# Layer 1 of a gated cross-attention stack: the last key tile joins the row sums on VectorE in about half of the groups

## The chip, the cores and the metric

The kernel runs on one core of one Trainium2 chip. The metric is the device time of one execution in microseconds (us); given is the median of several runs. Beside it there is one profiled execution, whose rows of instructions are used for all reasoning about single steps. In the profile PE is TensorE's matmuls, PEld its weight loads, DVE VectorE, ACT ScalarE, POOL GpSimd and SP the engine that issues most DMAs.

## The reference, cut to what matters

Two layers process 8 sequences of 512 tokens with 256 channels. Each layer is an attention part, gated with tanh(g) and added to x, and then a quantized feed-forward part. The change lies in the attention of layer 1, which has 16 heads of width 32 and two blocks for each sequence: a1 (self attention, with the mask applied after the softmax) and a2 (cross attention on the context, no mask):

```python
a = jax.nn.softmax(jnp.einsum('bhsd,bhtd->bhst', q, k) * D ** (-0.5), axis=-1)
if causal:
    mask = (jnp.arange(t)[None, :] > jnp.arange(s)[:, None]).astype(a.dtype)
    a = a * mask
o = jnp.einsum('bhst,bhtd->bhsd', a, v)
```

The softmax is normalized over all 512 keys, also in the masked block. So for each query and head the kernel needs the sum of 512 exponentials, and separately the product of the exponentials, masked or not, with v. Behind each block follow a product with li1, a layer norm, and an MLP of width 1024 (li2, GELU, li3).

## The kernel before, in words

**Groups.** Four heads make a group, so each of the 16 blocks (8 sequences times a1 and a2) has four groups, 64 in all. Scores are computed transposed: keys on the partitions, queries along the row. A group runs over four tiles of 128 keys (n = 0 to 3; last to first in a1). Each tile has two steps in `steps1` (line 2532):

- `front` (line 2547): four score products on PE, one per head, into two double banks of PSUM (line 2555); two exponentials of 128 x 1024 on ACT into a tile pt of 128 x 4 x 512 (line 2558). In a1, POOL also makes dg, a masked copy of the diagonal 128 columns (line 2562), and only the unmasked columns left of it and dg are multiplied with v.
- `back` (line 2570): the products of v with the parts, four heads side by side on the array (line 2579), into the bank ov. Beside them DVE gathers the row sums: at n = 1 it adds the tiles of n = 0 and 1 into acc (line 2587), at n = 2 it adds the third (line 2589). At n = 3 the sum over the partitions is made on PE: a product of acc with a matrix of ones, and a second of the last pt with ones, into one bank sm (lines 2593 to 2596). DVE turns sm, takes the reciprocal, spreads it and scales ov into oT (lines 2602 to 2607).

The ring of pt has three tiles (`PTS`), acc has one. Three PSUM banks (pool m1a, line 2100) serve all other products of layer 1, the bank sm among them; they come free when ACT or DVE has read them.

**The order.** PE, ACT, DVE, POOL and SP each run one fixed order, made when the program is built. `weave_all` (line 2152) keeps the attention steps and a number of streams: `first` and `last` (feed-forward parts of layers 0 and 1), `pair1` (queries and keys of a group), `pre1` (norms and values), `mlp1`, `keys2_rest` (keys and values of the context) and some small ones. Each has a due place counted in blocks: a base, plus a share of its work done. `Pace` (line 812) models when each engine is free and each tile done. Of the candidates that could start now, or within `soon`, the one with the smallest due place is issued next; if there is none, the one that can start first. Fronts are at most two ahead of backs. `back_at` (line 2611) says when a back may start; for n = 3 it is when pt, v and acc are done and a bank is free. All bases and shares stand in `SET`, `FIRST_AT` and `LAST_AT` (lines 29 to 74); `weave_timed` (line 1229) does the same for layer 0. Where PE would stand idle for long, `warm` (line 1282) puts in products that nobody reads.

**The keys of the context.** `keys2` (line 2025) makes keys and values of the first `KEYS_FIRST` sequences (five) during the feed-forward part of layer 0, and `keys2_rest` (line 2036) the others in layer 1, in tiles of the pt ring. Each takes eight products, eight evacuations, two stores to DRAM on SP's queue (lines 2068 and 2076) and a load from POOL's queue (lines 2022 and 2049). `mlp1` and the loads of the values wait until all are made.

Of the kernel before, what the change touches and what calls it, by code (L numbers as in the profile page):

```python
# [11 lines left out]
ALU = mybir.AluOpType  # L12
# [6 lines left out]
NT = T // P  # L19
# [6 lines left out]
MAGIC = 12582912.0  # L26
NEG = -1.0e30
ROWS = ((0, 1), (2, 3, 4), (5, 6, 7))
FIRST_AT = (-2.25, -0.57, 3.08, 3.44, 3.8, 6.44, 6.45, 6.2)
LAST_AT = (4.16, 6.04, 7.56, 7.63, 10.89, 12.49, 15.6)  # L30
PTS = 3
SET = dict(
    pairs0=2.7,
    post0=0.793,
    values0=0.0,
    few0=0.334,
    load1=1.367,
    norm0=0.547,
    ctx0=1.479,
    next0=1.066,  # L40
    gains_at=0.873,
    ready_at=-0.998,
    keys0=8.15,
    ease=1.612,
    zact=1.28,
    hold=0.158,
    keys0_at=-0.077,
    range_total=8.18,
    range_share=0.949,
    warm=0.888,  # L50
    conv_at=-1.687,
    soon=0.467,
    change0=0,
    change1=0,
    first=1.293,
    first_lag=4.549,
    last=0.367,
    last_total=7.836,
    last_lag=0.711,
    mlp0=0.488,  # L60
    mlp1=0.767,
    mlp0_at=1.131,
    mlp1_at=1.351,
    pre=1.286,
    pre_at=-1.524,
    pre_lag=0.783,
    pair=0.189,
    pair_at=-0.254,
    keys=0.466,
    keys_at=-0.443,  # L70
    back=1.031,
    tail_at=15.68,
    half_at=0.13,
)
KEYS_FIRST = 5


_COLS = [
# [995 lines left out]
class Fast(General):  # L1074
# [789 lines left out]
    def layer0_ffn(self):  # L1864
# [5 lines left out]
        with (  # L1870
# [18 lines left out]
            for b in range(B):  # L1889
                streams.append(Stream(self.ready0(b), 1.0, 0.1, b + SET["ready_at"]))  # L1890
                streams.append(Stream(self.range0(b), SET["range_total"], SET["range_share"], b))
            streams.append(Stream(self.chain(*(self.keys2(b) for b in range(KEYS_FIRST))), 64.0, SET["keys0"], SET["keys0_at"]))
            self.weave_timed([], streams)
# [131 lines left out]
    def keys2(self, b):  # L2025

        work, w = self.work, self.w1s[1]
        cT = self.cTs.pop(0)
        if b + 3 < KEYS_FIRST:
            self.load_cT(b + 3)  # L2030
# [5 lines left out]
    def keys2_rest(self):  # L2036
# [9 lines left out]
        def load(b):  # L2046
            if b < B:
                cTs[b] = self.early.tile([P, 1, T], F32, tag=f"x3T{b % 2}", name="cT")
                nc.gpsimd.dma_start(cTs[b][:, 0, :], self.cd[b])

        load(KEYS_FIRST)
        load(KEYS_FIRST + 1)
        yield WAIT
        for b in range(KEYS_FIRST, B):
            k = work.tile([P, 4, T], F32, tag="pt", name="k2", bufs=PTS)
# [34 lines left out]
    def layer1_xattn(self):  # L2090
        nc, tc = self.nc, self.tc
        with (
# [24 lines left out]

            for k, b in zip(FIRST_AT, range(B)):
                few.append(Stream(self.first(b), 3.8, SET["first"], k, SET["first_lag"]))
                if b == 1:  # L2120
                    few.append(Stream(self.load_mlp(), 1.0, 1.0, k))
            for k, b in zip(LAST_AT, range(B - 1)):
                few.append(Stream(self.last(b), SET["last_total"], SET["last"], k, SET["last_lag"]))
# [18 lines left out]
            self.keys_done, self.x0_read = False, 0  # L2142
            keys = [Stream(rest, 8.0 * (B - KEYS_FIRST), SET["keys"], SET["keys_at"])]
            self.weave_all(
# [387 lines left out]
    def steps1(self, b, blk):  # L2532

        nc, work, q, pace = self.nc, self.work, self.seqs[b], self.pace
        strict = blk == 0
        order = list(reversed(range(NT))) if strict else list(range(NT))
        slot = self.slot_of(b, blk)
        st = {}  # L2540

        def front_at(g):
            if ("QK", blk, g) not in q or slot and ("vt", blk) not in q:
                return 1e9
            return max(pace.when([Pace.name(t) for t in q["QK", blk, g]]), pace.place("st", 2))

        def front(g, n):
            kt = order[n]
            self.fronts += 1
            QT, KT = q["QK", blk, g]  # L2550
            diag = slice(kt * P, (kt + 1) * P)
            pss = [self.st.tile([P, 2, T], F32, tag="st", name="ps_s") for _ in range(2)][::-1]
            for j in (2, 3, 0, 1):
                r = slice(32 * j, 32 * j + 32)
                self.mm(pss[j // 2][:, j % 2, :], KT[r, diag], QT[r, :])
            pt = work.tile([P, 4, T], F32, tag="pt", name="pt", bufs=PTS)
            for jp in (1, 0):
                nc.scalar.activation(pt[:, 2 * jp : 2 * jp + 2, :], pss[jp], AF.Exp)  # L2558
            parts = [(pt, slice(0, T))]
            if strict:  # L2560
                dg = work.tile([P, 4, P], F32, tag="dg", name="dg", bufs=2)
                nc.gpsimd.affine_select(  # L2562
                    out=dg, in_=pt[:, :, diag], compare_op=ALU.is_gt, fill=0.0,
                    base=0, pattern=[[0, 4], [-1, P]], channel_multiplier=1,
                )
                parts = [(pt, slice(0, kt * P))] if kt else []
                parts.append((dg, diag))
            st[g, n] = (kt, pt, parts)

        def back(g, n):  # L2570
            self.backs += 1
            kt, pt, parts = st.pop((g, n))
            if n == 0:
                st["ov"] = self.ovp.tile([P, T], F32, tag="ov1", name="ov")
            ov = st["ov"]
            for i, (p, cols) in enumerate(parts):
                for j in (2, 3, 0, 1):
                    h = 4 * g + j
                    self.mm(
                        ov[32 * j : 32 * j + 32, cols], q["vt", blk][:, kt, 32 * h : 32 * h + 32],  # L2580
                        p[:, j, : cols.stop - cols.start],
                        n == 0 and i == 0, n == NT - 1 and i == len(parts) - 1,
                    )

            if n == 1:
                st["acc"] = work.tile([P, 4, T], F32, tag="acc", name="acc")
                nc.vector.tensor_tensor(st["acc"], st["pt"], pt, ALU.add)  # L2587
            elif n == 2:
                nc.vector.tensor_tensor(st["acc"], st["acc"], pt, ALU.add)  # L2589
            st["pt"] = pt  # L2590
            if n < NT - 1:
                return
            sm = self.bank()
            for k, t in enumerate((st["acc"], pt)):
                for j in (2, 3, 0, 1):
                    self.mm(sm[32 * j : 32 * j + 32, :], self.ones, t[:, j, :], k == 0, k == 1)

            if g == 0:
                st["recs"] = work.tile([P, 4, 16], F32, tag="recs", name="recs", bufs=2)
            rec = st["recs"][:, g, :]  # L2600
            rt = work.tile([P, 16, 32], F32, tag="rt", name="rt", bufs=1)
            nc.vector.transpose(rt.rearrange("p b d -> p (b d)"), sm)
            nc.vector.reciprocal(rec, rt[:, :, 0])
            rb = work.tile([P, T], F32, tag="rt", name="rb", bufs=1)
            nc.vector.transpose(rb, rec.unsqueeze(2).to_broadcast([P, 16, 32]))
            oT = q["oT", blk, g] = work.tile([P, T], F32, tag="oT", name="oT", bufs=5)
            nc.vector.tensor_tensor(oT, ov, rb, ALU.mult)  # L2607
            if g == 3:
                self.seen(st["recs"])

        def back_at(g, n):

            if n == NT - 1 and min(self.li1s) < (4 * slot + g - 1) // 4 or ("vt", blk) not in q:
                return 1e9
            _, pt, parts = st[g, n]
            t = pace.when([Pace.name(pt), Pace.name(q["vt", blk])] + [Pace.name(p) for p, _ in parts])
            if n == 0:
                return max(t, pace.place("ov1"))
            return max(t, pace.when([Pace.name(st["acc"])]), pace.place("m1")) if n == NT - 1 else t

        return [
            (lambda g=g: front_at(g), lambda g=g, n=n: back_at(g, n),
             lambda g=g, n=n: front(g, n), lambda g=g, n=n: back(g, n))
            for g in range(4) for n in range(NT)
        ]
# [337 lines left out]
```

## Time and profile before

| what | before |
|---|---|
| median of the runs | 2548.03 us (2546.71 to 2550.03, 3 runs) |
| profiled execution, its own time | 2552.98 us |
| its span, first to last instruction | 2551.2 us |
| mean granted TensorE clock | 0.98 of full speed |
| records of matmuls of pt with ones | 512, mean 606 ns |
| records of matmuls of acc with ones | 512, mean 607 ns |
| adds into acc on DVE | 64 of 2356 ns and 64 of 2419 ns in the mean |
| masked copies dg on POOL | 128, mean 1003 ns |

One product of four heads leaves eight matmul records, so 512 records are 64 groups. A row names the source line, the engine, the operation, "out<-in" by the program's names, the shapes and the count. A helper's line stands for all its callers: matmuls carry the lines of `mm` (1211 and 1215). In a row, "busy, mean" are the summed time and the mean of one; "<-" names what ended the idle time before it. Rows of the timeline begin with the start and the length in us.

### The profile page before, as it was taken

What the parts mean: (1) busy time and instruction counts of PE and PEld (TensorE: products, weight loads), DVE (VectorE), ACT (ScalarE), POOL (GpSimd) and SP (SyncE); (2) the same over time, 40 slices, a digit from 0 to 9 for tenths busy, and PEclk for the clock granted to TensorE, in tenths of its full rate; (3) what the DMA queues carried; (4) which work ended last, traced back from release to release, by engine and by line L of the source; (5) the groups of instructions that cost most, each with busy time, mean ns of one, the idle gap of its engine ahead of it and who ended that gap; (6) DMA issues with size and microseconds to landing.
All of it is one profiled execution on the core that took longest, in us unless ns stands there. A gap on an engine that the chain in (4) does not pass through costs nothing.

```text
span 2551.2 us, 68484 instructions
## 1 busy us (share of the span) xinstructions
PE 2401.7 (94%) x30510; PEld 1018.0 (40%) x30510; DVE 1718.6 (67%) x3118; ACT 1457.3 (57%) x1744; POOL 645.8 (25%) x684
## 2 busy tenths in 40 slices
PE   9999999999979998999999999999999989999975
PEld 3333333333423343334444434444444444344543
DVE  5544555444685656574877786778877877777867
ACT  5666776666685555555555555565555554565421
POOL 1211121111432444231423332222323441111100
PEclk9999999999999999999999999999999999999988
DMA  3101120000284302301201012331020102201000
GB/s 123 39 18 55 55 80 26 19 29 18 105 366 162 125 10 92 113 31 48 83 31 51 10 58 84 133 109 34 31 83 16 35 18 72 80 27 50 27 27 19
DMA packets 70640, 165.36 MB, mean 65 GB/s; under 512 B 5952, under 2 KB 32960, under 8 KB 63296
## 3 DMA queue, kind: packets, MB, share of 16 engines
q1 hardware_dynamic: 68960, 157.18, 17.7%
q8 instruction: 241, 3.95, 0.6%
q0 software_dynamic: 1088, 3.67, 0.5%
q14 instruction: 63, 0.52, 0.1%
q10 hardware_dynamic: 288, 0.05, 0.0%
HBM read 100.06 MB, written 60.82 MB: 63 GB/s over the span
## 4 chain that ended last, share of the span: by engine, by line


## 5 line engine op out<-in xcount | busy, mean ns | idle before, releaser
L2558 ACT ACTIVATE pt<-ps_s 128x1024 f32<-128x1024 f32 x512 | 496.2, 1021 | 342.5 <-PE ps_s L1215 257.4
L1215 PE MATMUL ps_s<-QT,KT 32*128 32x512 f32 (+3 forms) x4096 | 590.0, 598 | 22.6 <-ACT pt L2558 11.7
L1675 ACT ACTIVATE pt<-ps_s 128x1024 f32<-128x1024 f32 (+1 forms) x448 | 406.1, 961 | 198.7 <-PE ps_s L1215 191.9
L1215 PEld LDWEIGHTS ps_s<-QT,KT 32*128 32x128 f32 x4096 | 195.5, 183 | 352.0 <-issue 194.9
L1211 PE MATMUL ps<-x3T,li 128*32 128x256 f32 x4096 | 244.6, 384 | 5.4 <-DVE x3T L2483 4.2
L1211 PE MATMUL ps<-li,hD 128*32 128x256 f32 x4096 | 234.8, 382 | 2.0 <-ACT hD L2505 2.0
L1215 PE MATMUL ov<-pt,v 128*32 128x512 f32 (+3 forms) x2048 | 225.5, 522 | 5.6 <-POOL pt L1678 5.6
L2562 POOL TENSOR_SCALAR_AFFINE_SELECT dg<-pt 128x512 f32<-128x512 f32 x128 | 128.3, 1003 | 393.9 <-ACT pt L2558 392.1
L2315 POOL TENSOR_SCALAR mv<-mv 128x2 f32<-128x2 f32 (+1 forms) x104 | 67.0, 644 | 624.2 <-DVE mv L2310 620.2
L1215 PE MATMUL ov<-pt,vt 128*32 128x512 f32 (+3 forms) x1792 | 195.5, 508 | 13.1 <-DVE oT L2607 12.3
L1678 POOL TENSOR_SCALAR_AFFINE_SELECT pt<-pt 128x512 f32<-128x512 f32 (+1 forms) x96 | 83.1, 869 | 389.4 <-ACT pt L1675 389.4
L1211 PEld LDWEIGHTS ps<-li,hD 128*32 128x32 f32 x4096 | 130.5, 110 | 108.1 <-issue 14.8
L1211 PEld LDWEIGHTS ps<-x3T,li 128*32 128x32 f32 x4096 | 128.7, 111 | 110.5 <-issue 22.9
L2589 DVE TENSOR_TENSOR acc<-acc,pt 128x2048 f32<-128x2048 f32 x64 | 154.8, 2419 | 2.1 <-ACT pt L2558 1.5
L2587 DVE TENSOR_TENSOR acc<-pt 128x2048 f32<-128x2048 f32 x64 | 150.8, 2356 | 1.2 <-ACT pt L2558 1.2
L2082 ACT ACTIVATE hD<-ps,cols 128x256 f32<-128x256 f32 x131 | 57.6, 471 | 132.3 <-PE ps L1211 115.6
L1211 PE MATMUL ps<-zT,a_wq 128*32 128x512 f32 x1024 | 123.7, 602 | 2.4 <-DVE zT L2399 1.7
L1211 PE MATMUL ps<-li,oT 128*32 128x256 f32 x2048 | 123.0, 380 | 2.0 <-DVE oT L2607 1.3
L1701 DVE STREAM_TRANSPOSE ot<-ov 128x512 f32<-128x512 f32 x64 | 45.7, 714 | 109.3 <-PE ov L1215 109.3
L2681 DVE SCALAR_TENSOR_TENSOR hF<-hp,cols,hF 128x256 f32<-128x256 f32 x176 | 90.7, 515 | 27.8 <-ACT hF L2672 22.8
L1215 PEld LDWEIGHTS ov<-pt,v 128*32 128x32 f32 x2048 | 49.2, 108 | 148.0 <-issue 91.8
L2316 POOL TENSOR_TENSOR mv<-mv,mhalf 128x2 f32<-128x2 f32 (+1 forms) x120 | 99.6, 830 | 10.0
(350 smaller groups left out, 3562.6 us busy)
## 6 DMA issues: line engine op xcount, KB each, us to landing
hd<-h SPq DMA_DIRECT2D x14, 1024.0 KB, 6.7
hF<-hd SPq DMA_DIRECT2D x14, 1024.0 KB, 6.6
li<-in_w_a_dram SPq DMA_DIRECT2D x12, 1024.0 KB, 5.0
xF<-xd SPq DMA_DIRECT2D x21, 512.0 KB, 3.6
kd<-k SPq DMA_DIRECT2D x8, 1024.0 KB, 5.3
vd<-v SPq DMA_DIRECT2D x8, 1024.0 KB, 6.1
res<-rd SPq DMA_DIRECT2D x32, 256.0 KB, 2.8
vt<-vd SPq DMA_DIRECT2D x8, 1024.0 KB, 5.5
```

Source lines behind the costliest of these rows:

```text
L1211: self.nc.tensor.matmul(out[j : j + 32], lhsT[:, j : j + 32], rhs, start=start, stop=stop, skip_group_check=True)
L1215: self.nc.tensor.matmul(out, lhsT, rhs, start=start, stop=stop, skip_group_check=True)
L1675: nc.scalar.activation(pt[:, 2 * jp : 2 * jp + 2, :at], pss[jp][:, :, :at], AF.Exp)
L1678: nc.gpsimd.affine_select(out=diag, in_=diag, compare_op=ALU.is_ge, fill=0.0, base=0, pattern=[[0, 4], [0, len(kts)], [1, P]], channel_mul ...
L2082: self.nc.scalar.activation(out, ps, AF.Identity, bias=bias)
L2315: nc.gpsimd.tensor_scalar(rstd, mv[:, :, 1], EPS, None, ALU.add)
L2316: nc.gpsimd.tensor_tensor(rstd, rstd, self.mhalf[:, :nt], ALU.pow)
L2558: nc.scalar.activation(pt[:, 2 * jp : 2 * jp + 2, :], pss[jp], AF.Exp)
L2562: nc.gpsimd.affine_select(out=dg, in_=pt[:, :, diag], compare_op=ALU.is_gt, fill=0.0, base=0, pattern=[[0, 4], [-1, P]], channel_multiplier=1,
L2587: nc.vector.tensor_tensor(st["acc"], st["pt"], pt, ALU.add)
L2589: nc.vector.tensor_tensor(st["acc"], st["acc"], pt, ALU.add)
L2681: nc.vector.scalar_tensor_tensor(a, hp[:, half + k : half + k + n], self.col("conv_w", 3 * f + k), a, ALU.mult, ALU.add)
```

## The change

A new step `fold` adds the last pt into acc on DVE. It is tried twice: when the front of n = 3 has been issued, and after the add of n = 2. It needs both to have been issued, and it is done only if, by the plan's model, the add could start less than 3.5 us after the time at which PE becomes free. Where it was done, only acc is multiplied with ones; otherwise the two products remain. Which groups are folded is so decided when the program is built. The back of n = 3 may be issued 0.951 us before acc is done by the model. Nearly all numbers of the order are new, and `KEYS_FIRST` is 4, so one sequence's keys move to `keys2_rest`.

```diff
-FIRST_AT = (-2.25, -0.57, 3.08, 3.44, 3.8, 6.44, 6.45, 6.2)
-LAST_AT = (4.16, 6.04, 7.56, 7.63, 10.89, 12.49, 15.6)
+FIRST_AT = (-3.49, -0.02, 1.23, 2.56, 3.8, 6.79, 6.79, 6.17)
+LAST_AT = (3.99, 4.61, 6.9, 8.97, 11.78, 11.79, 15.6)
 SET = dict(
-    pairs0=2.7,
+    ones_lead=0.951,
+    ones_at=-3.5,
+    pairs0=3.004,
...
-    range_total=8.18,
-    range_share=0.949,
-    warm=0.888,
+    range_total=10.676,
+    range_share=1.373,
+    warm=0.656,
...
-    keys=0.466,
-    keys_at=-0.443,
+    keys=0.57,
+    keys_at=0.432,
...
-KEYS_FIRST = 5
+KEYS_FIRST = 4
...
             st[g, n] = (kt, pt, parts)
+            if n == NT - 1:
+                fold(g)
+
+        def fold(g):
+            if (g, NT - 1) not in st or st.get("folded") != (g, False):
+                return
+            pt = st[g, NT - 1][1]
+            at = pace.when([Pace.name(pt), Pace.name(st["acc"])])
+            if max(pace.free["DVE"], at) < pace.free["PE"] - SET["ones_at"]:
+                nc.vector.tensor_tensor(st["acc"], st["acc"], pt, ALU.add)
+                st["folded"] = g, True
...
                 nc.vector.tensor_tensor(st["acc"], st["acc"], pt, ALU.add)
+                st["folded"] = g, False
+                fold(g)
...
-            for k, t in enumerate((st["acc"], pt)):
+            terms = (st["acc"],) if st["folded"][1] else (st["acc"], pt)
+            for k, t in enumerate(terms):
                 for j in (2, 3, 0, 1):
-                    self.mm(sm[32 * j : 32 * j + 32, :], self.ones, t[:, j, :], k == 0, k == 1)
+                    self.mm(
+                        sm[32 * j : 32 * j + 32, :], self.ones, t[:, j, :],
+                        k == 0, k == len(terms) - 1,
+                    )
...
-            return max(t, pace.when([Pace.name(st["acc"])]), pace.place("m1")) if n == NT - 1 else t
+            return max(t, pace.when([Pace.name(st["acc"])]) - SET["ones_lead"], pace.place("m1")) if n == NT - 1 else t
```

More of the change, by code (lines that the diff above doesn't have):

```diff
@@ L28 @@
 ROWS = ((0, 1), (2, 3, 4), (5, 6, 7))
-FIRST_AT = (-2.25, -0.57, 3.08, 3.44, 3.8, 6.44, 6.45, 6.2)
-LAST_AT = (4.16, 6.04, 7.56, 7.63, 10.89, 12.49, 15.6)
+FIRST_AT = (-3.49, -0.02, 1.23, 2.56, 3.8, 6.79, 6.79, 6.17)
+LAST_AT = (3.99, 4.61, 6.9, 8.97, 11.78, 11.79, 15.6)
 PTS = 3
 SET = dict(
-    pairs0=2.7,
-    post0=0.793,
+    ones_lead=0.951,
+    ones_at=-3.5,
+    pairs0=3.004,
+    post0=0.995,
     values0=0.0,
[L36 to L39, printed above, removed]
+    few0=0.314,
+    load1=1.481,
+    norm0=0.045,
+    ctx0=2.216,
     next0=1.066,
[L41 to L47, printed above, removed]
-    range_total=8.18,
-    range_share=0.949,
-    warm=0.888,
-    conv_at=-1.687,
-    soon=0.467,
+    gains_at=0.94,
+    ready_at=-0.991,
+    keys0=8.019,
+    ease=1.509,
+    zact=1.418,
+    hold=0.54,
+    keys0_at=0.086,
+    range_total=10.676,
+    range_share=1.373,
+    warm=0.656,
+    conv_at=-1.489,
+    soon=0.459,
     change0=0,
     change1=0,
-    first=1.293,
-    first_lag=4.549,
-    last=0.367,
+    first=1.28,
+    first_lag=6.683,
+    last=0.301,
     last_total=7.836,
-    last_lag=0.711,
+    last_lag=0.672,
     mlp0=0.488,
@@ L63 @@
     mlp1_at=1.351,
-    pre=1.286,
-    pre_at=-1.524,
+    pre=1.139,
+    pre_at=-1.432,
     pre_lag=0.783,
-    pair=0.189,
+    pair=0.186,
     pair_at=-0.254,
-    keys=0.466,
-    keys_at=-0.443,
-    back=1.031,
-    tail_at=15.68,
+    keys=0.57,
+    keys_at=0.432,
+    back=1.001,
+    tail_at=15.748,
     half_at=0.13,
 )
-KEYS_FIRST = 5
+KEYS_FIRST = 4
 _COLS = [
```

## The prediction

> **What bounds the kernel now.** The page's head and its first two parts come first: which engine is busiest, and in which part of the span.
>
> ```profile
> span 2551.2 us, 68484 instructions
> PE 2401.7 (94%) x30510; PEld 1018.0 (40%) x30510; DVE 1718.6 (67%) x3118; ACT 1457.3 (57%) x1744; POOL 645.8 (25%) x684
> ...
> PE   9999999999979998999999999999999989999975
> DVE  5544555444685656574877786778877877777867
> ```
>
> PE is full nearly everywhere. DVE (VectorE) takes 4 or 5 tenths in layer 0 and 7 or 8 in layer 1. The chain of waits is empty in this profile, so busy times by stage take its place (start:end, length, then busy us per engine, granted clock, DMA):
>
> ```profile
> 0.00:660.00 660.00, 647.30 (x6590) 231.71 (x6594) 330.00 (x737) 440.96 (x499) 119.64 (x150) 1.00 0.14 46
> 660.00:800.00 140.00, 120.54 (x1428) 49.92 (x1424) 109.80 (x143) 99.05 (x156) 53.44 (x69) 0.93 0.66 263
> 800.00:2395.00 1595.00, 1522.43 (x20517) 669.04 (x20517) 1160.23 (x1989) 881.49 (x1023) 461.02 (x447) 0.99 0.18 59
> 2395.00:2551.00 156.00, 111.46 (x1994) 67.37 (x1983) 118.58 (x252) 35.77 (x67) 11.71 (x19) 0.87 0.08 25
> ```
>
> The third row holds all 64 groups of layer 1. PE idles 1595 - 1522.4 = 72.6 us in it (5%), DVE 434.8 us (27%). PE is the bound there, though not alone. The waits of PE in that stage say for whom (us in total, times, longest):
>
> ```profile
> PE ov L1215 <- POOL dg L2562: 15.6, 16, 3.1
> PE ov L1215 <- DVE oT L2607: 12.3, 15, 1.3
> PE ps_s L1215 <- ACT pt L2558: 11.7, 20, 1.8
> ```
>
> All rows on DVE together make about 36 us. No one wait is long: taking PE work away should shorten the span unless new waits fill the hole.
>
> **What is removed.** The end of one group on PE, from the timeline (start, length):
>
> ```profile
> 1656.85 1.03 PE L1215 MATMUL ov<-pt,vt 128*32 128x512 f32 x8
> 1657.70 1.03 PE L1215 MATMUL ps<-acc,ones 128*32 128x512 f32 x8
> 1658.56 1.03 PE L1215 MATMUL ps<-pt,ones 128*32 128x512 f32 x8
> ```
>
> The price is not the 1.03 us of the row, since neighbours overlap, but the distance between starts: 0.86 us. A folded group loses the third row. "About half" I take as 32 of 64: 32 x 0.86 = 27.5 us of PE (28 to 38 groups: 24 to 33). To see whether half is credible I read in the timeline, for each group, the end of its last exponential, the end of its second add, and the start of the product with acc. The second add ends after the exponential in 59 of 64 groups (median 1.8 us), so DVE has just become free. A further add of 2.35 us would end before the present start of the first sum product in 38 groups, and at most 2.05 us after it in the other 26. Half is what fits without delay.
>
> **What is added.** 32 more adds. Their cost is that of the two existing adds (ns, min/median/max):
>
> ```profile
> L2587 DVE TENSOR_TENSOR acc<-pt x64: 2257/2283/3357, 814.2 to 2379.4; 128x2048 f32<-128x2048 f32 x64
> L2589 DVE TENSOR_TENSOR acc<-acc,pt x64: 2257/2281/3365, 816.6 to 2383.5; 128x2048 f32<-128x2048 f32 x64
> ```
>
> The mean of L2589 on the page is 2419 ns, so 32 x 2.42 = 77 us, and DVE goes from 1160 to 1237 us of 1595, 78%. It has the room, and the cover is the PE work woven between exponential and sum (median 5.4 us). What leaks through:
>
> (a) DVE takes its work in order. The new add waits for the second exponential of the last key tile; behind it stand evacuations of the three banks, for which PE waits. Below nothing is possible only through the planner's other choices, which (c) holds. The low end is 0. The high end is a full add per fold, 32 x 2.28 = 73 us. Nearest row: 36 us of PE waits on 1160 us of DVE work, 0.031 us per us; 77 us would give 2.4 us. Waits grow faster than load, so I double it: +5 us.
>
> (b) In the self-attention block (half the groups, so some 16 folds) the mask's copy dg on POOL is released by the same exponential as the new add. An existing collision:
>
> ```profile
> 1999.53 2.28 DVE L2587 TENSOR_TENSOR acc<-pt 128x2048 f32<-128x2048 f32 x1
> 1999.73 2.58 POOL L2562 TENSOR_SCALAR_AFFINE_SELECT dg<-pt 128x512 f32<-128x512 f32 x1 [2.55 <-ACT pt L2558]
> ```
>
> The select's median is 635 ns, here it ends 0.5 us after the add. The Trainium skill (SBUF — State Buffer, section "SBUF: two separate sides") speaks against the change: a VectorE instruction with two SBUF inputs and a GpSimd one that reads SBUF exclude each other for the whole instruction. By the rule, with the add always first, an estimate of 16 x 2.28 = 36 us of POOL delay; by the page's row for these selects (mean 1003 against the median 635, so 0.37 us each) it is 6 us. But the sum has to wait for the add anyway, and the masked product before it takes some 0.2 us, so PE sees only the 0.5 us by which the select outlasts the add: at most 16 x 0.7 = 11 us. Ends 0 and 11, taken +3 us.
>
> (c) The settings are new and reorder everything, layer 0 too. The amount of work is the same but for KEYS_FIRST: one sequence's cross-attention keys and values (8 products of 0.86 us, 8 evacuations of 0.6 to 0.7 us, two stores of 1 MB on SP's queue, one load of cT from POOL's queue, 0.5 us to issue there) move from the end of layer 0 into layer 1. They pass, on SP, the loads of h and KT; on POOL, the first masks. At 749 to 757 us PE does such products while DVE works on the h extremes without a pause from 736.6 to 765.2, so their removal there saves nothing; in layer 1 they cost up to 6.9 us, or nothing where they fill the 9 us that PE idles between 800 and 900. Ends 0 and 6.9, taken +3. For the reordering as such I have no row; the settings move work, they don't make any. It is worth 0 here, -12 to +12 for the range (a sixth of the stage's 72.6 us of idle time).
>
> **The sum.** -27.5 + 5 + 3 + 3 = -16.5 us. The profiled execution took 2552.98 us (span 2551.2 and 1.8 around it), 4.95 us over the median 2548.03. A profiled 2536.5 then stands for a median of 2531.5 us. Spread of the likeliest case: 2521 to 2542.
>
> **Rivals.** (1) *The order gets better too*: with more slack on PE the weave also loses 12 us of idle time, near 2519. For it: PE idles 72.6 us in small pieces. Against: DVE becomes the harder engine to please. (2) *The hole is filled*: PE already waits beside the product (dg, oT, pt), or the gate opens in only 16 groups: 16 x 0.86 = 13.8 us, less 4 for (a) and (b) and 6.9 for the keys: -3, so 2545. For it: the waits above stand near the ends of groups. Against: 38 groups have room. (3) *VectorE's queue closes in front of PE*, and the kernel becomes slower. An add put into the queue when the scores are issued waits for them: in the timeline scores started at 1643.96 have their second exponential done at 1647.07, so 3.1 us, and with the add 5.4 us in which DVE evacuates nothing behind it. Three banks last PE 3 x 0.9 = 2.7 us; then it stands for 2.7. If that comes in half of the folds: 16 x 2.7 = 43 us against 27.5, with (b) and (c) +22, so 2570. It decides from a mean stall of 0.67 us per fold, (27.5 - 6)/32. For it: DVE waits on PE for 59 us at L2602, so it stands close behind PE. Against: DVE's last add mostly ends after the exponential, so the wait for the exponential is mostly covered. (4) That hardly any group folds belongs to (2).
>
> **Chances.** Likeliest 0.57 (2521 to 2542), rival 1 0.16 (2508 to 2521), rival 2 with 4 0.11 (2543 to 2553), rival 3 0.16 (2554 to 2585). About 0.2% (5 us) is what a measurement of this kernel can tell from no change. So faster 0.57 + 0.16 = 0.73, same 0.11, slower 0.16. Range 2512 to 2560: it leaves out a third of rival 1 and most of rival 3, some 0.17.
>
> **What would show it.** Matmul records of ps<-pt,ones fall from 512 by 8 per fold; a third line of acc adds appears with as many instructions, each 2.3 to 2.5 us. PE busy falls by about 27 us in all (here modelled rows of 1.03 us overlap, the union counts). PE's idle time in the layer-1 stage grows to about 80 us. If rival 3 holds, PE's waits on DVE rows (or on banks) grow by 40 us; with rival 2 the count of folds is small or the waits on dg and pt double. The prediction is wrong if the folds are far from 32, or if the stage between 660 and 800 us, which the folds don't touch, moves by over 10 us either way.

## The result, and the profile after

The changed kernel takes 2606.86 us (2605.67 to 2610.9, 4 runs) against 2548.40 us of the kernel before on the same chip: ratio 1.0232, 95% interval 1.0215 to 1.025, so 2.3% or 59 us slower. The forecast was 2531.5 us with a range up to 2560: it was wrong in its sign. The profiled execution took 2610.9 us, at a mean TensorE clock of 0.969 (before 0.980).

The head of the page and the tenths of PE and DVE:

```profile
span 2609.2 us, 68371 instructions
PE 2415.0 (93%) x30406; PEld 1027.4 (39%) x30406; DVE 1772.6 (68%) x3113; ACT 1472.1 (56%) x1779; POOL 653.0 (25%) x688
...
PE   9999999999978798999999999999999998999975
DVE  5554555443785566675877886767778777788886
```

PE has less to do and is busy 13 us longer. The rows of work, by line (busy time, mean ns, idle time before and who ended it), show that the change did what it says. First two rows of the kernel before, then the changed kernel:

```profile
L2558 ACT ACTIVATE pt<-ps_s 128x1024 f32<-128x1024 f32 x512 | 496.2, 1021 | 342.5 <-PE ps_s L1215 257.4 <-DVE acc L2587 47.1 <-issue 14.6
L1215 PE MATMUL ps<-acc,ones 128*32 128x512 f32 x512 | 68.4, 607 | 0.0
```

```profile
L2560 ACT ACTIVATE pt<-ps_s 128x1024 f32<-128x1024 f32 x512 | 496.2, 1021 | 317.3 <-PE ps_s L1217 195.1 <-DVE acc L2600 77.2 <-issue 25.3
...
L2580 DVE TENSOR_TENSOR acc<-acc,pt 128x2048 f32<-128x2048 f32 x35 | 84.9, 2425 | 4.9 <-ACT pt L2560 1.6
...
L1217 PE MATMUL ps<-acc,ones 128*32 128x512 f32 x512 | 69.3, 614 | 15.7 <-DVE acc L2580 15.0 <-ACT QT L2434 0.5 <-PE ov L1217 0.2
...
L1217 PE MATMUL ps<-pt,ones 128*32 128x512 f32 x232 | 30.7, 603 | 0.0
```

35 groups are folded: 232 records of the last product are left, 8 for each of 29 groups. The third line of adds is there at the price that was foreseen (2425 ns). The product of acc with ones, which before did not wait, waits 15 us for the third add. And the exponentials wait 77.2 us (before 47.1) for the first add, which frees a tile of the pt ring. By stage (start:end, length, busy us of PE, PEld, DVE, ACT, POOL, clock, DMA share, GB/s):

```profile
0.00:660.00 660.00, 647.29 (x6604) 231.97 (x6606) 328.99 (x735) 442.17 (x501) 119.60 (x150) 1.00 0.14 46
660.00:800.00 140.00, 119.91 (x1394) 49.50 (x1390) 109.36 (x142) 95.90 (x149) 55.72 (x73) 0.91 0.64 252
800.00:2395.00 1595.00, 1484.68 (x19634) 650.69 (x19630) 1168.44 (x1903) 863.82 (x1021) 463.23 (x445) 0.97 0.18 59
2395.00:2551.00 156.00, 133.49 (x2330) 77.17 (x2330) 128.72 (x267) 63.92 (x96) 14.05 (x20) 0.96 0.09 29
```

Up to 800 us nothing has moved. In the third row PE idles 110.3 us instead of 72.6, at a clock of 0.97 instead of 0.99. PE's waits between 800 and 2450 us (us in all, times, longest):

```profile
PE ps_s L1217 <- ACT pt L2560: 22.0, 26, 3.2
PE ps L1217 <- DVE acc L2580: 15.0, 11, 5.7
PE ov L1217 <- DVE oT L2626: 14.7, 13, 4.7
PE ov L1217 <- POOL dg L2564: 11.3, 12, 2.4
PE ps L1213 <- DVE x3T L2485: 8.0, 4, 3.1
```

All rows of this view together: 56.6 us for DVE (40.4 in the same stretch before), 35.9 for ACT (18.6), 11.3 for POOL (15.6). So two kinds of wait have grown, for VectorE and for the exponentials. Over the whole span PE idles 2609.2 - 2415.0 = 194.2 us (before 149.5), +45. The clock in the trace is either full or half; by its record PE is busy for 130 us at half clock, before 79, and half of the difference, 26 us, is an estimate of what the clock took. The products left out take 35 x 0.86 = 30 us off. That leaves 17 of the span's 58 us, among them some 4 for more of the products that keep PE busy in long pauses (414 records, before 262).

When the sum of each group starts tells where the delay arises: +23 us against before at group 3, +37 at group 10, +41 at 24, +48 at 40, +60 at 52, +51 at the last. Two thirds are there after eleven groups.

### The profile page after: what moved, and what is told of

The parts are those of the page before. It is cut to its first block, busy times and chain, and to the rows that moved or that the text cites. A ratio compares the mean times of both kernels' runs of the same rounds, so it can differ in the third digit from the quotient of the medians.

```text
span 2609.2 us, 68371 instructions
## 1 busy us (share of the span) xinstructions
PE 2415.0 (93%) x30406; PEld 1027.4 (39%) x30406; DVE 1772.6 (68%) x3113; ACT 1472.1 (56%) x1779; POOL 653.0 (25%) x688
## 5 line engine op out<-in xcount | busy, mean ns | idle before, releaser
L1217 PE MATMUL ps_s<-QT,KT 32*128 32x512 f32 (+3 forms) x4096 | 605.2, 604 | 33.7 <-ACT pt L2560 22.0
L1213 PE MATMUL ps<-x3T,li 128*32 128x256 f32 x4096 | 251.0, 390 | 11.4 <-DVE x3T L2485 8.0
L2317 POOL TENSOR_SCALAR mv<-mv 128x2 f32<-128x2 f32 (+1 forms) x104 | 57.5, 553 | 665.7 <-DVE mv L2312 665.1
L2602 DVE TENSOR_TENSOR acc<-acc,pt 128x2048 f32<-128x2048 f32 x64 | 148.9, 2327 | 7.8 <-ACT pt L2560 7.1
```

Of the source, the lines that this page charges most:

```text
L1213: self.nc.tensor.matmul(out[j : j + 32], lhsT[:, j : j + 32], rhs, start=start, stop=stop, skip_group_check=True)
L1217: self.nc.tensor.matmul(out, lhsT, rhs, start=start, stop=stop, skip_group_check=True)
L2317: nc.gpsimd.tensor_scalar(rstd, mv[:, :, 1], EPS, None, ALU.add)
```

## The experiments

The theory after this profile: an add put into VectorE's queue delays what stands behind it, and PE waits for that; beside it the new settings cost by themselves. Rivals: the settings cost everything, without folds; GpSimd is shut out by the add's two SBUF operands; the folds stand in the wrong groups. In the runs called "order of before" every engine's instructions stand as in the kernel before, but for those added or dropped; the plan counts a dropped instruction as if it were issued and doesn't count an added one. Differences in us are (ratio - 1) x 2548.4, so that all have one base, with the 95% interval behind.

**The parts of the change.** *Settings alone*: the changed kernel with `ones_at=1e9, ones_lead=0.0`, so that no group folds. The lead of 0.951 us is out with the folds.

> The changed kernel with the gate shut (ones_at=1e9, ones_lead=0), so new settings and KEYS_FIRST 4, no folds, planned anew. If the new settings carry the 47 us that the changed order costs without its folds, 2585 to 2605 us. If the planner's answer to the folds carries most of it, 2550 to 2570 us.

Ratio 1.0085: +21.7 us (17 to 27). *Keys back*: the changed kernel with folds, but

```diff
-KEYS_FIRST = 4
+KEYS_FIRST = 5
-    keys=0.57,
-    keys_at=0.432,
+    keys=0.466,
+    keys_at=-0.443,
```

> The changed kernel with KEYS_FIRST, keys and keys_at as before, planned anew. If the keys moved into the first groups of layer 1, which are short of other work, cost there (the changed kernel is 23 us behind at the fourth group), this gains 10 to 20 us: 2585 to 2597. If the folds in those groups are the cause, at most 8 us: 2598 or more.

Ratio 1.0131: +33.4 (28 to 39), 26 us less than the whole change and more of a gain than either expectation had. *Settings with keys back*, no fold:

> The changed kernel's settings without any fold (2570.3 us), but the five-sequence part of the keys before layer 1 as in the kernel before (KEYS_FIRST 5 and its two settings). If the moved keys are all that the settings cost: 2546 to 2553. If the other settings cost by themselves: 2558 to 2570.

Ratio 1.005: +12.7 (8 to 18), inside the second expectation. Its sums run level with before up to group 43 and are 31 us late at group 48, 14 at the end: the other settings cost there. *Keys alone*: the kernel before with the edit of "keys back" turned round.

> The kernel before with only the keys moved: KEYS_FIRST 4 and its two settings (keys, keys_at) as in the changed kernel, no fold, the plan made anew. If one more sequence's keys in layer 1 cost by themselves what the runs with and without them differ by (9 us without folds, 21 us with): 2555 to 2572. If they cost only in company of the other settings: 2543 to 2553.

Ratio 1.005: +12.7 (8 to 17). The sums are +9 us late at group 3, +14 at group 4, and +8 to +13 from there to the end. Its timeline says how (start, length; in brackets the idle time before and its releaser; the value tiles are L1541's rows):

```profile
844.83 1.94 ACT L2558 ACTIVATE pt<-ps_s 128x1024 f32<-128x1024 f32 x2 [4.90 <-DVE acc L2587]
846.66 0.59 ACT L1541 COPY v<-ps 128x512 f32<-128x512 f32 x1
...
858.81 0.59 ACT L1541 COPY v<-ps 128x512 f32<-128x512 f32 x1
...
864.85 1.94 ACT L2558 ACTIVATE pt<-ps_s 128x1024 f32<-128x1024 f32 x2 [5.45 <-DVE acc L2587]
```

and on PE:

```profile
845.91 2.99 PE L1215 MATMUL ps_s<-QT,KT 32*128 32x512 f32 x8 [3.09 <-ACT pt L2558]
...
865.93 2.99 PE L1215 MATMUL ps_s<-QT,KT 32*128 32x512 f32 x8 [4.50 <-ACT pt L2558]
```

The values of the last sequence lie in a tile of the pt ring while the copies of 839 to 859 us fill it (its store is issued at 859.4, before at 792.4). Groups 2 and 3 have two tiles instead of three; the exponentials wait until an add frees one, and the scores wait for the exponentials. The same waits are in the changed kernel (3.17 us at 853.59). This is read from the trace; no run gives the keys tiles of their own.

**The folds.** *In the order of before*, at the groups that the change's rule picks (32):

```diff
+                pace.mute = True
+                nc.vector.tensor_tensor(st["acc"], st["acc"], pt, ALU.add)
+                pace.mute = False
...
+                    if k and folded:
+                        pace.ghost("PE", made[i], Pace.name(sm), [Pace.name(self.ones), Pace.name(pt)])
+                        continue
```

> The order of every engine is that of before, instruction for instruction; only 32 of the 64 groups get the third add on DVE, where the gate of the change opens on this order, and lose their product of the last tile with ones. If the new order is what costs the time (the planner's answer to the change, and the new settings), then this is at most as slow as before: 32 x 0.86 = 27 us less on PE, 5 to 15 us of new waits, so 2525 to 2540 us. If the add itself stands in the way of each group's end (exponential, add, sum, then the single bank ov comes free), each fold costs 2.3 us less 0.86, and this takes 2590 us or more.

Ratio 1.011: +28.0 (23 to 33), between the two expectations. *The order of the changed kernel without its folds* (35 adds out, 35 products back):

> The order of every engine is that of the changed kernel, instruction for instruction; its 35 third adds are taken out of DVE's order and the 35 products of the last tile with ones put back on PE. If the order is what costs, this stays near the changed kernel: 35 x 0.86 = 30 us more on PE, some of it in gaps, so 2600 to 2625 us. If the adds cost by delaying what waits for them, it falls to 2550 to 2575 us.

Ratio 1.0185: +47.1 (41 to 53), just under the first expectation. So the order made around the folds, lead included, costs 47.1 - 21.7 = 25 us more than the one that the same settings make without them, and the folds on top of it only the 12 us left of the 59. *Folds with the settings of before*, the order made anew (33 folds; `ones_lead` stays at 0.951):

> The settings of before with KEYS_FIRST 5, and the change's code for the fold, planned anew. If the fold, with the planner's answer to it, is the cause, this is as slow as the changed kernel or slower, 2590 to 2620 us. If the new settings are the cause, it is 2525 to 2545 us.

Ratio 1.0204: +52.0 (47 to 57), 24 us more than the folds in the old order.

**What one add costs.** The next runs keep the order of before. *Reads only*: in the 32 groups of the first fold run VectorE takes a max over the last pt (2.28 us, result unused), and both products stay.

```diff
+                nc.vector.tensor_reduce(self.waste, pt.rearrange("p j t -> p (j t)"), AX.X, ALU.max)
```

> The order of before; in the same 32 groups as in the run with folds on that order DVE gets, at the place of the add, a maximum over the last tile into a column that nobody reads; both products with ones remain, so the output is the reference's. It costs DVE about the same time and waits for the same exponential, but nobody waits for its result. If DVE's load and its closed queue are the cost, 2570 us or more (1 us for each of 32). If only what waits for the sum costs, 2550 to 2558 us.

Ratio 1.0068: +17.3 (12 to 23), between the two expectations, 0.54 us per read. The folds in the same places cost (28.0 + 22.7)/32 = 1.6 us each, with the saving measured below, in other groups, added back. So in the places of the change's rule the queue alone makes a third of a fold's price. What a fold has beside it shows in PE's waits of that run: 11.6 us for the add before the sum (here none), and 24.3 for dg (here 15.2). The select's mean is 1091 ns there and 997 here: in these places the add with two SBUF operands does hold GpSimd up more than the read with one, and PE waits some 9 us longer for it. *Roomy groups*: folds in the 32 groups with most room between last exponential and sum (5.8 us or more); *tight groups*: in the other 32.

> The order of before; folds in the 32 groups in which, in the profile of before, the longest time lies between the last exponential and the first product with ones (5.8 us and more). If a fold costs by its place, where the sum follows the exponential closely, these are nearly free: -27 us on PE, 5 to 10 us of DVE's waits, 2527 to 2540 us. If DVE's load or the shared order costs per fold whatever its place, it is about as slow as the first run with 32 folds: 2565 to 2580 us.

> The order of before; folds in the other 32 groups (5.0 us or less from the last exponential to the sum). If place decides: each costs up to 2.3 us and gives 0.86, so 32 x 1.4 = 45 us more, 2585 to 2600 us. If cost doesn't depend on the place: 2565 to 2580 us, the same as with the 32 roomy groups.

Ratios 1.017 (1.0153 to 1.0187) and 1.0174 (1.0157 to 1.0191): +43 and +44. My expectation for the roomy groups was wrong on the other side of zero. No sum waits for its add there, and it costs as much as where 24 of 32 sums do. *Reads in the roomy groups*:

> The instruction order of the kernel before on every engine. In the same 32 groups with the longest room in which a run folded before (2591.9 us), VectorE gets, in the place of the add, a max over the last tile of exponentials (128x2048, some 2.3 us, one SBUF operand, its result not used, nobody waits for it); both products with ones stay. Theory A (the length of the instruction in VectorE's in-order queue is what costs): the add there cost PE (2591.9 - 2548.4 + 27.5)/32 = 2.2 us each, and the read should cost nearly as much, so 2600 to 2620. Theory B (an add with two SBUF operands shuts GpSimd out, and its late layer-norm and mask steps cost): a read with one operand doesn't, so at most a third of it, 2550 to 2575. The sum's wait for acc can't play a part in either.

Ratio 1.0184: +46.9 (41 to 54), 1.47 us per read. Nothing uses the result, and the product with ones still reads the tile after it, so what is left is its place in the queue. One of these reads, step by step. First the kernel before, PE's timeline:

```profile
1773.77 1.46 PE L1211 MATMUL ps<-zT,a_wk 128*32 128x512 f32 x12
1775.06 0.39 PE L1211 MATMUL ps<-xq,fw 128*32 128x257 bf16 x8
1775.28 3.63 PE L1211 MATMUL ps<-li,hD 128*32 128x256 f32 x64
1778.73 0.39 PE L1211 MATMUL ps<-xq,fw 128*32 128x257 bf16 x8
```

And on DVE:

```profile
1777.84 0.74 DVE L2084 TENSOR_SCALAR KT<-ps,a_wk_b 128x512 f32<-128x512 f32 x1
```

PE runs through without a pause. The last product needs the bank of the first, which DVE empties into KT until 1778.58, 0.15 us before PE is ready for it. Now the run with the reads, 24.2 us later:

```profile
1797.95 1.46 PE L1234 MATMUL ps<-zT,a_wk 128*32 128x512 f32 x12
...
1799.46 3.63 PE L1234 MATMUL ps<-li,hD 128*32 128x256 f32 x64
1799.81 2.28 DVE L2626 TENSOR_TENSOR acc<-acc,pt 128x2048 f32<-128x2048 f32 x1
...
1802.01 2.28 DVE L2603 TENSOR_REDUCE waste<-pt 128x1 f32<-128x2048 f32 x1
...
1804.21 0.74 DVE L2107 TENSOR_SCALAR KT<-ps,a_wk_b 128x512 f32<-128x512 f32 x1
...
1805.00 0.40 PE L1234 MATMUL ps<-xq,fw 128*32 128x257 bf16 x8 [1.92 <-DVE KT L2107]
```

The read starts at once and waits for nothing. It moves the evacuation behind it by 2.2 us, the bank comes free 2.2 us later, and PE stands 1.92 us. From here on everything runs 2.2 us later. A read that starts at 1700.79 costs nothing. It stands where VectorE, in the kernel before, waits twice for PE (its timeline):

```profile
1677.98 0.48 DVE L2514 SCALAR_TENSOR_TENSOR res<-ps,gate,res 128x256 f32<-128x256 f32 x1 [1.15 <-PE ps L1211]
1678.38 0.15 DVE L2319 SCALAR_TENSOR_TENSOR mv<-mv 128x2 f32<-128x2 f32 x1
1682.63 0.48 DVE L2514 SCALAR_TENSOR_TENSOR res<-ps,gate,res 128x256 f32<-128x256 f32 x1 [4.09 <-PE ps L1211]
```

The two short instructions come late, and the pause of 4.09 us takes the delay up.

*Pieces*: as in the roomy groups, but each add cut into four of 128x512, one between each two of VectorE's next instructions.

> The instruction order of the kernel before, folds in the same 32 roomy groups as the run at 2591.9 us, but each add is cut into four of 128x512 (some 0.69 us each), one between each two of VectorE's next instructions, so that nothing behind waits for more than one piece at a time. Theory A (one long instruction closes the queue; VectorE's idle time comes in pauses of about 1.1 us, into which pieces fit): most of the 43 us goes, 2535 to 2560. Theory D (VectorE has no free time that is really free, each us of added work is passed on): 4 x 0.69 = 2.8 us per fold instead of 2.4, so 2590 to 2605.

Ratio 1.0175 (1.0151 to 1.0199): +45, no better than whole. The pieces take 789 ns each (128 of them), 3.2 us per fold, and seven sums now wait for their last piece, 8.1 us in all. So cutting did not help; whether shorter instructions would cost less at the same total, this run can't tell. *The saving alone*: in the roomy groups the product is dropped and nothing is added (the last tile is missing from those sums).

> The instruction order of the kernel before. In the 32 roomy groups the product of the last tile with ones is left out and nothing is added on VectorE (the sum of those rows lacks the last tile's exponentials). This is the saving alone. If TensorE sets the pace there, 32 x 0.86 = 27.5 us come off: 2518 to 2526. If TensorE waits for VectorE's chain in those places anyway, the hole is filled: a third or less, 2539 to 2549.

Ratio 0.9911 (0.9888 to 0.9933): -22.7 us, 0.71 per product. *The add alone*: third add and both products (the last tile counts twice).

> The instruction order of the kernel before. In the 32 roomy groups the third add is made and both products with ones are kept as well (the last tile is counted twice in those rows' sums). With the run of the read in the same place (1.0184), this tells a two-operand add from a one-operand read with all else the same. Queue time alone: as the read, 2588 to 2602. The add's two operands shutting GpSimd out as a cost of its own: about 20 us more, 2608 to 2625.

Ratio 1.023 (1.0206 to 1.0253): +58.6, between the two expectations, so 1.83 us per add of 2.45. Against the read it is 12 us more (interval some 3 to 21), of which 5.6 are the longer instruction (32 x 0.176). What two operands may add in these groups by shutting GpSimd out is not told from zero: PE's waits for dg are 15.7 us with the adds, 15.6 with the reads and before. *VectorE relieved*: the second add is left out in the roomy groups (their sums lack the third tile), the products stay.

> The instruction order of the kernel before, with VectorE's work taken off instead of added: in the 32 roomy groups the second add (third tile) is left out and nothing replaces it (the sum of those rows lacks the third tile); both products stay. If VectorE sets the pace around these groups as much as TensorE does, an add less gives back what an add more costs, some 1.4 us each: 2498 to 2515. If TensorE sets the pace and the written order merely leaves VectorE's results no slack, little comes back: 2530 to 2548.

Ratio 0.9958 (0.9945 to 0.9971): -10.7 us. An add more costs 1.83 us, an add less gives 0.33, though the one taken out stands earlier in the queue than the one put in.

**Folds in pauses.** *Twelve whole adds*, each where VectorE pauses for 2 us or more by the planned times, and *fourteen*, one of them in four pieces. The second numbers count VectorE's instructions up to the place of the add:

```diff
+FOLDS = {5: 961, 9: 1062, 15: 1206, 21: 1436, 25: 1576, 33: 1798, 35: 1854, 43: 2143, 49: 2388, 53: 2525, 59: 2692, 8: 1040}
...
+        if self.pace.count in self.pace.due:
+            self.pace.due.pop(self.pace.count)()
```

> The instruction order of the kernel before. Whole adds in only 12 groups, each put where VectorE's queue has, by the planned times, a pause of 2 us or more between the last exponential and the group's sum; the product with ones is left out there. Theory A (queue length): the add fits in the pause, and PE saves 12 x 0.86 = 10 us: 2536 to 2545, faster than both kernels. Theory C (whatever lies behind the add is delayed by its full length anywhere, the pauses are not where the plan has them): 12 x (2.2 - 0.86) = +16, so 2560 to 2568.

> The instruction order of the kernel before. Folds only where VectorE's queue pauses by the planned times: 14 groups (13 whole adds, two of the earlier 12 moved to a longer pause and one group added; one more group in four pieces of 128x512, each in a pause of 0.75 us or more). With 12 such folds 7.4 us came off (0.9971). If a fold in a pause costs nothing, 14 x 0.86 = 12 us come off: 2534 to 2540. If only the best pauses are free, about as with 12: 2540 to 2544.

Ratios 0.9971 (0.9961 to 0.998) and 0.996 (0.9942 to 0.9978): -7.4 and -10.2 us, both faster than the two kernels given, and not told apart. Twelve products at 0.71 are 8.5 us, fourteen 9.9: in a pause an add costs next to nothing. All twelve groups are among the roomy ones, where the adds stood elsewhere in the queue; there, from the sum before to the sum of these twelve groups, the delay against before grew by 24 us in all, here it fell by 3. So it is the place in the queue that decides, not the group. The row of the twelve, with no stretched one among them:

```profile
L2602 DVE TENSOR_TENSOR acc<-acc,pt 128x2048 f32<-128x2048 f32 x12 | 27.4, 2280 | 0.1
```

## Why the prediction was wrong

Two terms of its sum failed, both far too small: step (a), what an add costs in VectorE's queue (5 us foreseen, some 37 by what the runs give), and in step (c) the order, put at 0 (25 measured for the order made around the folds). The saving and step (b) were about right, and the keys cost four times what was taken for them.

**What is removed** was right in size: 35 groups folded (28 to 38 foreseen), 22.7 us measured for 32 products (17 to 28.5) against 27.5.

**"Half is what fits without delay"** was the first step that failed. It asked whether the add ends before the sum that needs it. With that question answered yes in all 32 groups (roomy), folding cost as much as with it answered no. There the next instruction in VectorE's queue decides, often an evacuation that has nothing to do with the group. In the places of the change's rule both count: 0.54 us of queue in the 1.6 us of a fold.

**Step (a), "+5 us"**, is the mis-sized term. It took PE's waits per us of VectorE work, 0.031, as the price of a further us; that is an average over work for which the order has already been arranged. The price of a further us is 1.83 / 2.45 = 0.75 us for the adds in the roomy groups, 24 times as much; for the reads in the places of the rule it is 0.54 / 2.28 = 0.24, still 8 times. The upper bound in the text (a full add per fold, 73 us) was near the 58.6 measured; I chose by the wrong row. "It has the room", by DVE's 27% idle time, failed with it: the idle time of 800 to 2395 us comes in some 350 pauses of over 0.1 us, worked out from the trace, only 36 of them as long as the add; and the fixed order lets PE use many results just as they are done, as KT above, so that a push is passed on even where a pause follows. That it isn't VectorE's load as such is shown by taking load off (10.7 us came back, not 58.6) and by the adds in pauses, which cost next to nothing.

**Step (b), "+3 us"**, stayed inside its ends: with folds in the roomy groups the select's mean went from 1003 to 1039 ns, and PE's waits for dg didn't grow. Where the change's rule puts them, in the order of before, the mean is 1091 and those waits grew by 8.7 us, inside the upper end of 11 (16 x 0.7; with the 0.5 us that its line shows it would be 8); in the changed kernel they are 11.3 us, less than before.

**Step (c), "+3 us" for the keys and 0 for the order**, was too low on both. The keys cost 12.7 us alone, over the upper end of 6.9: I priced the products and evacuations, and not the tile of the pt ring that they hold. (The idle time of PE between 800 and 900 us, given as 9 us, is 8.4.) The other settings cost 12.7 and the order made around the folds 25, twice the 12 allowed.

The sum as measured: settings with keys 21.7, order around the folds 25, adds less products in it 12, together 59. The last term holds the saving: with 35 x 0.71 = 25 us off, the adds themselves cost some 37 us there, 1.05 each. That is less than in the order of before, so the parts can't be added freely across orders. Nor do the settings lose where the changed kernel does: up to group 43 settings with keys stand at +11, as much as the keys alone; then their sums jump by 36 us at group 48 and come back to +22, and the changed kernel has no such jump. At group 43 the same runs read 11 for the settings with keys, 32 for the order around the folds and 8 for the folds. Why the order made around folds is worse is open. It appears twice (24 and 25 us), both times with the lead of 0.951 us, which no run takes out alone, and in the changed kernel's order without folds it lies in the first twenty groups (+41 us at group 20, where the settings alone have +9), but no run changes one choice in it.

**Rival 3** named the right mechanism, VectorE's queue closing in front of PE, and its point of decision, 0.67 us per fold, lies below all folds outside pauses. Its account of the stall was too narrow: it wanted the add to wait for an exponential, and the read above waits for nothing. Of the signs announced, the stage of 660 to 800 us stayed (119.91 against 120.54), and the rows of VectorE grew by 16 us, not 40; the rest is ACT's exponentials and the clock. PE's idle time grew past the 80 us to 110.

## What to carry to other kernels

In a fixed, tight order the price of an instruction added to a second engine isn't its share of that engine's idle time. Look at what stands behind it in the queue and how soon the busy engine uses that; unless a pause of its length lies at that spot, a good part of its duration is lost (here between a quarter and three quarters), and less is regained when you remove one. When work is moved, price the buffers that it holds as well as its instructions.

## What was not expected of the hardware

The granted clock followed PE's pauses: between 850 and 900 us PE is busy 34.5 us at 0.86 in the changed kernel, 40.12 at 0.93 with the folds in the order of before, 45.06 at 0.97 before. It is at half in stretches of 3.4 us or a multiple. Between 800 and 2395 us the changed kernel has 18 of them and the kernel before 9, and each begins during a pause of PE or within 2.5 us after one. The shortest pause that stands alone before such a stretch took 1.26 us (from 2240.0, in the kernel before; half clock from 2243.2), but a pause of 2.91 us there (from 1077.7) has none behind it. Over the span the estimate above puts it at 26 us, a good two fifths of the loss. And a 128x512 add took 789 ns in the mean, so cutting one of 128x2048 into four makes 2.45 us into 3.2.
